# Moving a pair's second-layer weight loads to another queue, with four smaller reorderings around them

## Chip, cores and metric

The kernel runs on one core of a Trainium2 chip. The metric is the device time in microseconds of one execution; the times below are medians over repeated runs. The program's engines are TensorE (PE in the profile, its weight loads PEld), VectorE (DVE), ScalarE (ACT), GpSimd (POOL) and SyncE (SP). Transfers are issued from the queues of SP, POOL and, at the start, ACT.

## The reference

4096 tokens of width 256 pass a linear attention and a gated feed-forward block, each followed by a layer norm, in fp32:

```python
x = layernorm(x + attn(x))          # Q (K^T V) sqrt(3/D) Wo^T, D = 64
h = silu(x w1^T * s1) * (x w2^T * s2)        # 256 -> 1024
h = gelu(h h1^T * hs1)                        # 1024 -> 1024
h = gelu(h h2^T * hs2)                        # 1024 -> 1024
x = layernorm(x + (h w3^T) * s3)              # 1024 -> 256
```

The weights are ternary up to a scale.

## The kernel before

**Tiles and pairs.** The tokens are cut into 8 tiles of 512, and these are worked on in 4 pairs (tiles 0 and 1, 2 and 3, ...). An fp32 operand is split into a `hi` part (a cast, ScalarE) and a `lo` part (what the cast lost, VectorE), and TensorE runs every product twice, once with each. `convert` (L231, L232) does the split.

**A square layer.** The two 1024 x 1024 layers are computed for a pair at once by a scheme with 7 block products in place of 8 (`square_layer`). `product` issues 32 matmuls (L278) of 512 columns, about 7.25 us in all, into four PSUM banks: `al` or `be`. There are 14 products per pair, 7 per layer, counted in `products[0]` from 0. Their weight blocks are, in order, `A11, A12, S2, S1, S3, A22, S4`, each in two halves of 512 KB. `A11`, `A12` and `A22` are parts of the weight matrix itself; the `S` blocks are sums of its quarters. VectorE makes these sums once (`sums`, called per slice k = 0 to 3, in two halves `first` and `second`, through two rotating buffers named `so`), and POOL stores them into the DRAM arrays `sw` (L440). In the chain around a layer, `c11`, `c22` and `c12` add bank contents to a buffer on VectorE and apply a gelu on ScalarE; `c22` reads the four banks of `be` before product 6 adds to them.

**Weight queue.** `fetch` keeps up to five half blocks ahead (`HELD = 5`). For the first pair, `A` blocks of both layers come straight from the weight matrix on POOL's queue (L267); everything else comes from `sw` on SP's queue (L269). For the later pairs `copy` (L260) writes the `A` blocks from the matrix into `sw`, on SP's queue, after the products listed in `COPY`.

**Background work.** `fill(us)` gives out jobs from a list until a budget of microseconds is used up; a job may overdraw it, and what is overdrawn is taken from the next budget. The budgets of a layer are those after products 2, 3, 4 and 5 (`FIRST` in the first layer of the first pair, `FILL` elsewhere). In the first pair the list holds the sums of the second layer (`k0` to `k3`, two jobs of 1.4 each), for tiles 2 and 3 the normalisation (`a0, a1`, `b0, b1`, 1.3 each; statistics on VectorE, L167 on POOL) and the transposes (`a2, a3`, `b2, b3`, 0.8 each; VectorE, L815). `a3` and `b3` also put 32 small transfers into a list (`moves`, L216), which SP and POOL take in turn, up to 14 after each product.

**Around it.** Before the first pair, `stack_lo` (L550) makes the low parts of three stacked query tiles on POOL, and `attend_norm` normalises tiles 0 and 1 on VectorE (L167) with a root on POOL (L86). After each pair, `last_products` (L755) applies w3, and a dummy Silu on ScalarE fetches its table for the next pair. At the very end the kernel tests that its inputs are of the kind that it presumes (`within`, L863 and L864, a minimum, L998, and a matmul with ones, L1005), and branches on the outcome; the last normalisation is L1002.

[...]

Of the kernel before, what the change touches and what calls it, by code (L numbers as in the profile page):

```python
# [15 lines left out]
AF = mybir.ActivationFunctionType  # L16
ALU = mybir.AluOpType
AX = mybir.AxisListType
# [11 lines left out]
NP = NT // 2  # L30
NS = T // P
# [13 lines left out]
def block_kernel(ctx: ExitStack, tc: tile.TileContext, a: dict, out: bass.AP):  # L45
# [15 lines left out]
    nc = tc.nc  # L61
# [12 lines left out]
    mhalf = const("mhalf", [P, NS])  # L74
    once = const("once", [P, 1])
    ones = const("ones", [P, 1])
# [97 lines left out]
    def turn_on_pe(t, slot):  # L174

        hi, lo = slot
        j = t % 2

        def turn(s0, s1):
            for k in range(KE):  # L180
                for s in range(s0, s1):
                    nc.tensor.transpose(
                        aux[k][:, s * P : (s + 1) * P], x2[t][:, s, k * P : (k + 1) * P], ident
                    )

        def split(s0, s1):
            c = slice(s0 * P, s1 * P)
            for k in range(KE):
                h = hi[:, 2 * j + k, c]
                nc.scalar.copy(h, aux[k][:, c])  # L190
                nc.vector.tensor_tensor(  # L191
                    lo[:, 2 * j + k, c], aux[k][:, c], h.bitcast(F32), ALU.subtract
                )

        return turn, split
# [30 lines left out]
    def convert(src):  # L226

        hi, lo = next_slot()
        for h in range(2):
            c = slice(2 * h, 2 * h + 2)  # L230
            nc.scalar.copy(hi[:, c, :], src[:, c, :])  # L231
            nc.vector.tensor_tensor(  # L232
                lo[:, c, :], src[:, c, :], hi[:, c, :].bitcast(F32), ALU.subtract
            )
        return hi, lo

    MOVES = 14
    FILL = {2: 2.0, 3: 4.0, 4: 1.5, 5: 3.5}
    FIRST = {2: 2.8, 3: 5.4, 4: 2.8, 5: 5.4}

    PLACE = {A11: (0, 0), A12: (HK, 0), A22: (HK, T)}
    ORDER = [A11, A12, S2, S1, S3, A22, S4]
# [7 lines left out]
        return a[f"h{layer + 1}"][:, k0 : k0 + HK, c]  # L250


    copies = deque((layer, m, h) for layer in range(2) for m in PLACE for h in range(2))

    products = [0]
    COPY = (*range(8, 14), *range(15, 21))

    def copy():
        layer, m, h = copies.popleft()
        nc.sync.dma_start(out=sw[layer][m, h], in_=block(layer, m, h))  # L260

    def fetch(most=HELD):
        while wanted and len(held) < most:
            p, layer, m, h = wanted.popleft()
            w = p1.tile([P, HK, T // 2], FR, tag="ws", name=f"ws{m}", bufs=HELD)
            if p == 0 and m in PLACE:
                nc.gpsimd.dma_start(out=w, in_=block(layer, m, h))  # L267
            else:
                nc.sync.dma_start(out=w.bitcast(F32), in_=sw[layer][m, h])  # L269
            held.append(w)  # L270

    def product(ps, part, start):
        for h in range(2):
            w = held.popleft()
            for o in range(2):
                for k in range(HK):
                    for i in range(2):
                        nc.tensor.matmul(  # L278
                            ps[2 * h + o], w[:, k, o * P : (o + 1) * P], part[i][:, k, :],
                            start=start and k == 0 and i == 0, stop=k == HK - 1 and i == 1,  # L280
                            skip_group_check=True,
                        )
        fetch()
        products[0] += 1
        if products[0] in COPY:
            copy()
        move(MOVES)

    def plus(dst, u, v, op=ALU.add, engine=nc.vector):
# [2 lines left out]
    background = deque()  # L292
# [256 lines left out]
    def stack_lo(t):  # L549
        nc.gpsimd.tensor_tensor(  # L550
            stk[t][D:P], qf[t][D:P], stk[t][D:P].bitcast(F32), ALU.subtract
        )
# [3 lines left out]
    LATE = 6  # L556
# [42 lines left out]
    split(0, 2)  # L599
    norm(2)  # L600
    norm(3)
    for t in range(3, LATE):
        stack_lo(t)
    for t in range(LATE, NT):
        stack(t)

# [39 lines left out]
    for g in range(2):  # L646
        stats(g)
        root(g)
    turn, split = turn_on_pe(1, slot)
    for i in range(3, 2 * KH):  # L650
        for ps, w in zip(ring[i % 3], (w1, w2)):
# [8 lines left out]
        if i in (11, 14):  # L660
            t = 2 + i // 14
# [99 lines left out]
    def take(t, s, engine=nc.gpsimd):  # L761

        ps = (al, be)[t % 2][s]
        y = x2[t]
        d = p2.tile([P, E], F32, tag="d", name=f"d{t}", bufs=4)
        nc.vector.tensor_tensor(d, ps[:, :E], s3, ALU.mult)  # L766
        engine.tensor_tensor(y[:, s, :], y[:, s, :], d, ALU.add)  # L767
# [93 lines left out]
    def within(dst, var, so_far):  # L861

        nc.vector.tensor_scalar(dst, var, low, so_far, ALU.is_ge, ALU.mult)  # L863
        nc.vector.scalar_tensor_tensor(dst, var, high, dst, ALU.is_le, ALU.mult)  # L864
# [8 lines left out]
    for p in range(NP):  # L873
        ta, tb = 2 * p, 2 * p + 1
        if p > 0:
            first = []
            ask(1)
            for i in range(2 * KH):
                for ps, w in zip(ring[i % 3], (w1, w2)):
                    gate_products(ps, w, i % KH, slot, i // KH)  # L880
                if i == 0:
                    take(tb - 2, 0)
                    take(tb - 2, 1)
                if i == 1:
                    take(tb - 2, 2)
                    take(tb - 2, 3)
                gate(i, xb)
                if i in (2, 3, 5):
                    fill(1.2)
                if i in (4, 8):  # L890
                    first.append(convert(xb[0 if i == 4 else 2]))
                if p + 1 < NP and i in (6, 11):
                    t = ta + 2 + int(i == 11)
                    steps[t] = attend_norm(
                        t, xs[t], attention_out(t), (p2, late)[(p + 1) % 2]
                    )
                    steps[t][0](0)
                    steps[t][0](1)
                if i in (9, 10, 12, 13):
                    fill(1.2)  # L900
                if p == NP - 1 and i in (11, 13, 15):
                    bounds((i - 11) // 2)
        if p + 1 < NP:
            (a0, a1), (a2, a3) = attend_jobs(ta + 2)
            (b0, b1), (b2, b3) = attend_jobs(tb + 2)
            if p == 0:
                k0, k1, k2, k3 = (second_sums(k) for k in range(HK))
                background.extend((*k0, *k1, a0, a1, *k2, *k3, b0, b1, a2, a3, b2, b3))
            else:
                background.extend((a0, a1, b0, b1, a2, a3, b2, b3))  # L910
        tail = lambda: None
        for layer, sc in enumerate((hs1, hs2)):
            if p + layer > 0:
                ask(4 if p else 1)
            if p == NP - 1 and layer == 1:
                background.append((1.4, functools.partial(bounds, 3)))
            xb, first, tail = square_layer(
                xb, first, sc, tail, FILL if p + layer else FIRST
            )
        while background:  # L920
            background.popleft()[1]()
        if p + 1 < NP:
            nc.scalar.activation(once, mhalf[:, :1], AF.Silu)

        made = {}

        for s in range(NS):
            last_products(0, first[0], s)
        move(MOVES)
        tail()  # L930
        made[2] = convert(xb[3])
        for s in range(NS):
            last_products(1, first[1], s)
        move(MOVES)
        made[3] = convert(xb[1])
        for s in range(NS):
            take(ta, s)
        if p == NP - 1:
            break
        for i in (2, 3):  # L940
            for s in range(NS):
                last_products(i, made[i], s)
            if i == 2:
                move(len(moves))
                made[4] = convert(xTr)
        if p + 2 < NP:
            xs[ta + 4] = load_x(ta + 4)
            xs[tb + 4] = load_x(tb + 4)
        slot = made[4]
        xb = (xb[4], xb[5], xb[0], xb[2], xb[3], xb[1])  # L950
        background.extend(end_jobs(ta))
        background.extend(end_jobs(tb))
# [20 lines left out]
    g, v = nc.gpsimd, nc.vector  # L973
# [16 lines left out]
    for s in range(2):  # L990
        norm_on_act(tb, s, *rb[s])
    store(tb, 0, 2)
    take(tb, 3, v)
    rb.update(close(tb, [2]))
    norm_on_act(tb, 2, *rb[2])
    store(tb, 2, 3)
    within(ok[:, n - NS : n + 3], mvo[:, n - NS : n + 3, 1], fine)
    nc.vector.tensor_reduce(some, ok[:, : n + 3], AX.X, ALU.min)  # L998
    rb.update(close(tb, [3]))
    within(ok[:, n + 3 :], mvo[:, n + 3 :, 1], some)  # L1000
    y = x2[tb][:, 3, :]
    nc.vector.tensor_scalar(y, y, mvo[:, n + 3, 0:1], rb[3][1], ALU.subtract, ALU.mult)  # L1002
    store(tb, 3, 4)
    pf = bank[7][:1, :1]
    nc.tensor.matmul(pf, ok[:, n + 3 :], ones, start=True, stop=True)  # L1005
    nc.vector.tensor_scalar(flag, pf, float(P), None, ALU.is_lt)
    differs = nc.values_load(
        flag, engines=AGAIN, min_val=0, max_val=1,
# [156 lines left out]
```

## Time and profile before

| what | value |
| --- | --- |
| median of 3 runs | 652.41 us (651.53 to 653.03) |
| the profiled execution | 653.67 us, its span 651.9 us |
| TensorE busy | 631.8 us, 97% |
| VectorE, ScalarE, POOL busy | 496.1, 381.4, 233.1 us |
| DMA | 113.44 MB, mean 174 GB/s |

The span is the time from the first to the last instruction of the program, and the busy times are shares of it. In a row of instructions the columns are: start and length in us (timeline), or busy time in us, mean length of one in ns, and idle time before (groups); then engine, line and operation, what is written from what (buffer numbers left out), shapes, and the count. What stands in brackets, or behind `<-`, is what ended the idle time before. A row of the windows holds the window, its length, the busy time of the engine with its count of instructions, the granted TensorE clock as a share of full speed, the busy share of the DMA engines, and GB/s.

### The profile page before, as it was taken

To read this page: it belongs to the slowest core of one execution; us is meant where nothing else is said; L and a number is where in the kernel's file an instruction comes from. 1 tells how busy PE (TensorE), PEld (TensorE's weight loads), DVE (VectorE), ACT (ScalarE), POOL (GpSimd) and SP (SyncE) were. 2 spreads that over 40 slices of the span, in tenths; PEclk is the share of its full clock that TensorE was granted. 3 is DMA by queue.
4 is the path that set the end of the run, shared out by engine and by line. 5 is a ranking of instruction groups with operands and counts; after the bars stand their busy time and mean duration, and the time that the engine had idled before them with its cause. 6 is when DMAs were issued, how large, how long until landed. Compare 5 with 4: busy or idle time off the path is not lost.

```text
span 651.9 us, 8976 instructions
## 1 busy us (share of the span) xinstructions
PE 631.8 (97%) x3163; PEld 533.6 (82%) x3163; DVE 496.1 (76%) x750; ACT 381.4 (59%) x522; POOL 233.1 (36%) x290
## 2 busy tenths in 40 slices
PE   8999999959999999999999999999999999999994
PEld 7878888848898888888898888888899888888894
DVE  3789986895475888698677988798767987588466
ACT  5546472645664455655684556766684556766564
POOL 1234117722814713632535722631645720000005
PEclk9999999979999999999999999999999999999998
DMA  8988749845853037764762125654860125644201
GB/s 335 330 300 246 244 144 364 268 155 182 250 152 103 33 137 247 268 218 167 225 191 71 60 97 171 216 183 154 248 190 4 65 98 173 215 150 141 98 1 67
DMA packets 58800, 113.44 MB, mean 174 GB/s; under 512 B 19488, under 2 KB 34528, under 8 KB 58368
## 3 DMA queue, kind: packets, MB, share of 16 engines
q1 hardware_dynamic: 40864, 73.56, 34.0%
q0 software_dynamic: 17520, 38.55, 18.6%
q10 hardware_dynamic: 368, 0.72, 0.3%
q8 instruction: 26, 0.43, 0.3%
q14 instruction: 22, 0.18, 0.1%
HBM read 97.08 MB, written 18.87 MB: 178 GB/s over the span
## 4 chain that ended last, share of the span: by engine, by line
PE 86%; DMA 5%; DVE 5%; POOL 1%; issue 1%; ACT 1%; SPq 0%; POOLq 0%; DVEq 0%; ACTq 0%
PE bank L278 53%; PE bank L611 18%; PE bank L755 9%; DMA sw<-so 3%; PE bank L507 2%; DVE f L290 2%; PE bank L528 1%; DMA ws<-in_h 1%; POOL x L167 1%; DVE so L290 1%; DMA f<-in_xt 1%; PE bank L518 1%; PE bank L137 1%; PE bank L138 1%; DVE lo L232 1%
## 5 line engine op out<-in xcount | busy, mean ns | idle before, releaser
L278 PE MATMUL bank<-hi,ws 128*128 128x512 f32 x896 | 350.3, 391 | 7.7 <-DMA ws<-in_h 7.7
L278 PE MATMUL bank<-lo,ws 128*128 128x512 f32 x896 | 349.9, 391 | 0.0
L232 DVE TENSOR_TENSOR lo<-f,hi 128x1024 fp32r<-128x1024 f32 x144 | 170.3, 1221 | 69.6 <-ACT hi L231 69.1
L278 PEld LDWEIGHTS bank<-hi,ws 128*128 128x128 f32 x896 | 169.0, 189 | 43.3 <-DVE f L290 8.1
L278 PEld LDWEIGHTS bank<-lo,ws 128*128 128x128 f32 x896 | 169.1, 189 | 35.2
L231 ACT CAST hi<-f 128x1024 fp32r<-128x1024 f32 x144 | 144.5, 1051 | 52.0 <-PE bank L278 26.9
L318 ACT ACTIVATE f<-f,hs 128x512 f32<-128x512 f32 x96 | 62.8, 715 | 71.7 <-DVE f L290 71.7
L611 PE MATMUL bank<-hi,w 128*128 128x512 f32 (+1 forms) x268 | 101.7, 383 | 1.0 <-DVE d L766 0.6
L611 PE MATMUL bank<-lo,w 128*128 128x512 f32 (+1 forms) x268 | 101.2, 381 | 0.1
L620 ACT ACTIVATE f<-bank,s 128x512 f32<-128x512 f32 x64 | 44.0, 690 | 65.6 <-PE bank L611 62.3
L290 DVE TENSOR_TENSOR f<-f,f 128x1024 f32<-128x1024 f32 x64 | 76.5, 1221 | 4.5 <-ACT f L318 3.8
L290 DVE TENSOR_TENSOR f<-f,bank 128x512 f32<-128x512 f32 x96 | 62.1, 681 | 21.8 <-ACT f L371 16.0
L767 POOL TENSOR_TENSOR x<-x,d 128x256 f32<-128x256 f32 x31 | 27.0, 897 | 114.0 <-DVE d L766 113.9
L621 DVE SCALAR_TENSOR_TENSOR f<-bank,s,f 128x512 f32<-128x512 f32 x64 | 47.7, 748 | 26.2 <-PE bank L611 23.6
L755 PE MATMUL bank<-w,lo 128*128 128x256 f32 x256 | 61.6, 283 | 0.0
L755 PE MATMUL bank<-w,hi 128*128 128x256 f32 x256 | 61.6, 283 | 0.0
L611 PEld LDWEIGHTS bank<-hi,w 128*128 128x128 f32 x268 | 50.4, 188 | 11.3 <-DVE d L766 1.0
L611 PEld LDWEIGHTS bank<-lo,w 128*128 128x128 f32 x268 | 50.4, 188 | 9.6 <-DVE lo L191 0.3
L216 POOL DMA_DIRECT2D xT<-x x96 | 52.2, 551 | 8.1 <-DMA stage<-in_h 3.0
L755 PEld LDWEIGHTS bank<-w,lo 128*128 128x128 f32 x256 | 49.1, 192 | 0.2
L755 PEld LDWEIGHTS bank<-w,hi 128*128 128x128 f32 x256 | 49.1, 192 | 0.2
L717 POOL DMA_DIRECT2D stage<-in_h x16 | 9.0, 561 | 107.8 <-DVE stage L743 104.0
(121 smaller groups left out, 553.1 us busy)
## 6 DMA issues: line engine op xcount, KB each, us to landing
ws<-sw SPq DMA_DIRECT2D x100, 512.0 KB, 3.3
sw<-so POOLq DMA_DIRECT2D x16, 512.0 KB, 5.4
stage<-in_h POOLq DMA_DIRECT2D x16, 512.0 KB, 5.0
ws<-in_h POOLq DMA_DIRECT2D x12, 512.0 KB, 7.4
sw<-in_h SPq DMA_DIRECT2D x12, 512.0 KB, 5.5
x<-in_x SPq DMA_DIRECT2D x16, 256.0 KB, 3.7
f<-in_xt SPq DMA_DIRECT2D x6, 512.0 KB, 7.8
f<-in_h SPq DMA_DIRECT2D x6, 512.0 KB, 10.3
```

What stands on the lines that cost most here:

```text
L216: moves.popleft()()
L231: nc.scalar.copy(hi[:, c, :], src[:, c, :])
L232: nc.vector.tensor_tensor(lo[:, c, :], src[:, c, :], hi[:, c, :].bitcast(F32), ALU.subtract)
L278: nc.tensor.matmul(ps[2 * h + o], w[:, k, o * P : (o + 1) * P], part[i][:, k, :], start=start and k == 0 and i == 0, stop=k == HK - 1 and ...
L290: engine.tensor_tensor(dst, u, v, op)
L318: nc.scalar.activation(dst, src, AF.Gelu, scale=sc[:, o : o + 1])
L507: nc.tensor.matmul(pk[:, s, :], x[:, k, s * P : (s + 1) * P], wkv[:, k, :], start=(k == 0), stop=(k == KE - 1),)
L611: nc.tensor.matmul(ps[:, c], w[:, k, o * P : (o + 1) * P], part[:, 2 * j + k, c], start=(k == 0 and i == 0), stop=(k == KE - 1 and i == 1),)
L620: nc.scalar.activation(g, pa, AF.Silu, scale=s1[:, o : o + 1])
L621: nc.vector.scalar_tensor_tensor(g, pb, s2[:, o : o + 1], g, ALU.mult, ALU.mult)
L755: nc.tensor.matmul(ps[:, :E], part[q][:, k, s * P : (s + 1) * P], w3[:, k0 + k, :], start=i % 2 == 0 and k == 0 and q == 0, stop=i % 2 == ...
L767: engine.tensor_tensor(y[:, s, :], y[:, s, :], d, ALU.add)
```

## The change

- For the first pair, only the first layer's `A` blocks come on POOL's queue; the second layer's come from `sw` on SP's queue. The copies of the second layer are made first, and copies are given out at the start of products 0, 1, 2, 5, 7 to 12, 14 and 15.
- The budgets `FIRST` rise from 2.8 / 5.4 to 3.2 / 5.8, and in the list the transposes of tile 2 (`a2, a3`) stand ahead of the normalisation of tile 3 (`b0, b1`).
- `stack_lo` is issued behind the root of tile 1.
- The dummy Silu is issued behind `tail`, the last gelu of the pair.
- At the end, the last add of tile 3 is issued behind tile 2's normalisation and store, and the tests of the last tile are made in one step in place of two.

```diff
-    FIRST = {2: 2.8, 3: 5.4, 4: 2.8, 5: 5.4}
+    FIRST = {2: 3.2, 3: 5.8, 4: 3.2, 5: 5.8}
...
-    copies = deque((layer, m, h) for layer in range(2) for m in PLACE for h in range(2))
+    copies = deque((layer, m, h) for layer in (1, 0) for m in PLACE for h in range(2))
...
-    COPY = (*range(8, 14), *range(15, 21))
+    COPY = (0, 1, 2, 5, *range(7, 13), 14, 15)
...
-            if p == 0 and m in PLACE:
+            if p + layer == 0 and m in PLACE:
                 nc.gpsimd.dma_start(out=w, in_=block(layer, m, h))
...
     def product(ps, part, start):
+        if products[0] in COPY:
+            copy()
...
         products[0] += 1
-        if products[0] in COPY:
-            copy()
         move(MOVES)
...
     norm(3)
-    for t in range(3, LATE):
-        stack_lo(t)
     for t in range(LATE, NT):
         stack(t)
...
     for g in range(2):
         stats(g)
         root(g)
+    for t in range(3, LATE):
+        stack_lo(t)
...
-                background.extend((*k0, *k1, a0, a1, *k2, *k3, b0, b1, a2, a3, b2, b3))
+                background.extend((*k0, *k1, a0, a1, *k2, *k3, a2, a3, b0, b1, b2, b3))
...
-        if p + 1 < NP:
-            nc.scalar.activation(once, mhalf[:, :1], AF.Silu)
-
         made = {}
...
         tail()
+        if p + 1 < NP:
+            nc.scalar.activation(once, mhalf[:, :1], AF.Silu)
...
     store(tb, 0, 2)
-    take(tb, 3, v)
     rb.update(close(tb, [2]))
     norm_on_act(tb, 2, *rb[2])
     store(tb, 2, 3)
-    within(ok[:, n - NS : n + 3], mvo[:, n - NS : n + 3, 1], fine)
-    nc.vector.tensor_reduce(some, ok[:, : n + 3], AX.X, ALU.min)
+    take(tb, 3, v)
     rb.update(close(tb, [3]))
-    within(ok[:, n + 3 :], mvo[:, n + 3 :, 1], some)
+    within(ok[:, n - NS :], mvo[:, n - NS :, 1], fine)
+    nc.vector.tensor_reduce(some, ok, AX.X, ALU.min)
...
-    nc.tensor.matmul(pf, ok[:, n + 3 :], ones, start=True, stop=True)
+    nc.tensor.matmul(pf, some, ones, start=True, stop=True)
```

## The prediction, made before the changed kernel was run

> **What bounds the kernel now.** I read the page first (TensorE busy 97% of the span, so only what it waits for can be won), then the waits of TensorE:
>
> ```profile
> engine line waited for: us in total, times, longest us
> PE bank L278 <- DMA ws<-in_h: 7.7, 1, 7.7
> ...
> PE bank L182 <- DVE x L167: 0.7, 1, 0.7
> PE bank L611 <- DVE d L766: 0.6, 1, 0.6
> ```
>
> One wait matters: 7.7 us for a weight block (`ws<-in_h`, the loads on POOL's queue). The chain over 90 to 143 us tells why it is late:
>
> ```profile
> 115.93 5.08 DMA sw<-so
> ...
> 125.85 3.83 POOL x L167 x2
> ...
> 134.19 7.89 DMA ws<-in_h
> ...
> 142.21 1.19 PE bank L278 x2
> ```
>
> The load was queued on POOL behind tile 3's normalisations (L167) and issued only at 134.19. TensorE's windows show a second price:
>
> ```profile
> 136.00:137.00 1.00, 0.00 (x0) 1.00 0.88 287
> 137.00:138.00 1.00, 0.00 (x0) 0.52 1.22 337
> 143.00:147.00 4.00, 4.00 (x10) 0.50 0.02 4
> 147.00:148.00 1.00, 1.00 (x5) 0.86 0.00 0
> ```
>
> The granted clock (third figure) fell to half some 2.6 us into the wait and came back at about 147.3. The chain has 42.54 us for the 176 matmuls after the wait; at the 101.55 us that it has for 448 elsewhere, they take 39.9. So the wait costs 7.7 + 2.7 = 10.4 us. Two further readings decide what replaces it. VectorE's timeline:
>
> ```profile
> 112.84 0.69 DVE L290 TENSOR_TENSOR so<-xT 128x512 fp32r<-128x512 f32 x1 [0.98 <-DMA sw<-so]
> 113.44 0.69 DVE L290 TENSOR_TENSOR so<-xT,so 128x512 fp32r<-128x512 f32 x1
> 114.05 2.47 DVE L290 TENSOR_TENSOR f<-f,bank 128x512 f32<-128x512 f32 x4
> ...
> 121.13 0.69 DVE L290 TENSOR_TENSOR so<-stk 128x512 fp32r<-128x512 f32 x1 [0.47 <-DMA sw<-so]
> ```
>
> and POOL's:
>
> ```profile
> 106.32 1.63 POOL L86 TENSOR_TENSOR ra<-ra,mhalf 128x2 f32<-128x2 f32 x1
> ...
> 111.81 3.34 POOL L167 TENSOR_SCALAR x<-x,mv,ra 128x256 f32<-128x256 f32 x2
> 115.09 0.84 POOL L267 DMA_DIRECT2D ws<-in_h  x1
> 115.93 1.51 POOL L440 DMA_DIRECT2D sw<-so  x2
> ```
>
> The rows at 114.05 are `c22`, which reads the banks `be`; TensorE starts product 6, which writes them, at 116.2 (72.66 + 6 x 7.25), only 1.5 us after `c22(0)`. The row at 121.13 is the first half of the sums of k=3, waiting for the store of k=2 to free its buffer. That store left POOL at 115.93, behind tile 2's normalisations, and landed 5.08 us later.
>
> **Weights by copies.** Six POOL loads (0.75 to 0.9 us of issue, 7.4 us to landing) become SP loads (0.32 us, 3.3 us to landing). The copies they need go out at products 0, 1, 2, 5, 7, 8, and each lands in about 5.5 us (median of the 12); each is read at least one product (7.25 us) later. A12's second half can be issued when its buffer is free (about 120) instead of 134.19, and is wanted at 134.3. The 10.4 us go. What is late next in that line is S2 of this layer, which needs the sums of k=3 stored: wanted at product 9, not close. Extra traffic: three copies at about 69, 80 and 88 us, where the DMA engines are half busy (0.51 over 80 to 100), one at 109, where they are full.
>
> **Larger budgets.** `FIRST` of 3.2 / 5.8 lets `fill` give out: k0, k0, k1 after product 2; k1, tile 2's two norm jobs, k2 after product 3; k2 **and the first half of k3** after product 4; k3, both transposes of tile 2, both norm jobs of tile 3 and, by the rounding of the remainder, the first transposes of tile 3 after product 5. The half of k3 thus moves ahead of `c22`. It cannot start before k2's first store has landed:
> - k1's first half waits for the store landing at 100.65 as now, but the two `lo` of t4 (2.3 us) now stand behind it; k1's second half ends at about 105.7 instead of 104.1. POOL issues its store and two raw loads by 107.8 (now 106.3).
> - Tile 2's norm jobs take 8.8 us of POOL now (106.32 to 115.09), partly in VectorE's way; I take 7.6, since VectorE will stand still for their end: k2's store leaves at 115.4. Landing is 5.1 us now and 3.4 at the least for such stores; with the copy and three loads on SP's queue beside it I take 5.0: 120.4.
> - k3's half takes 1.4, `c22(0)` 0.7: TensorE starts product 6 at 122.6, not 116.2, a new wait of 6.4 us (bounds: 4.0 with 114.5 and 3.6; 8.0 with 116.6 and 5.5).
> - The clock: 2.7 us again. The Trainium skill (TensorE: Matmul & The Clock Gate, What's actually happening) says about 3.4 us of work restore it, which would be 1.7; the row has 5.1 us (142.2 to 147.3), and I use the row.
>
> Queued behind the half of k3 on VectorE: `c22`, the `lo` of n1, k3's other half, four transposes (0.33 each), tile 3's statistics, two transposes that wait for POOL's first norms of tile 3 (about 2.7), the `lo` of n2, `c12`, `both`, t2. Adding the rows' durations from the landing at R: `lo` of t2 ready and the first bank copied at R + 27.8, product 9 wants them at R + 26.5; `c11(0)` ends at R + 36.0, product 10 wants it at R + 35.1. Two more waits, 1.3 + 0.9 = 2.2 us (bounds 0 and 5).
>
> This part: -10.4 + 6.4 + 2.7 + 2.2 = **+0.9**.
>
> **Order on POOL of A22 and k1's store.** A22's second half now goes out behind k1's first store (103.2 instead of 98.95). By the queue's order they swap landings: 110.4 instead of 108.9; wanted at 112.5. Nothing; 1 us if the queue is slower.
>
> **Transposes of tile 2 ahead.** 32 small DMAs, 16 on each of POOL (0.55 us) and SP (0.6 us), 7 of each per product from product 6: about 4 us of 7.25 on each queue. SP's loads run four blocks ahead, which hides them (without that lead a block would come up to 4 us late); at the handover to pair 1, the xT wait goes that held ACT, then VectorE's L766, then TensorE by 0.6: **-0.6** (0 to -0.6). The Silu load behind `tail` saves two table loads of 1.28 us on ACT, none of which TensorE waits for: nothing.
>
> **`stack_lo` later.** Now, at 37.4 us:
>
> ```profile
> 37.44 2.75 DVE L167 TENSOR_SCALAR x<-x,mv,ra 128x256 f32<-128x256 f32 x2
> ...
> 50.38 1.45 DVE L167 TENSOR_SCALAR x<-x,mv,ra 128x256 f32<-128x256 f32 x4
> ```
>
> Two normalisations took 2.75 us beside the three `stack_lo` on POOL (37.47 to 41.3), while four took 1.45 at 50.38. Moving POOL's work away saves TensorE its waits of 0.74 and 0.18 at 40 us: -0.9. But it lands at 50.6, right behind POOL's root of tile 1 (49.88 + 0.69), where those four run, and TensorE's transposes follow at 51.44. The Trainium skill (SBUF — State Buffer, Who interferes with whom) speaks against this: the pair of ports is locked for a whole instruction and issue order decides. If VectorE, which starts at 50.38, kept it through, nothing would be lost; but at 37.44 VectorE started 30 ns ahead and still lost, so by the row three of the four wait 1.3 us each and the last ends at 54.7 instead of 51.9: +2.8. I take +2.8; the clock should hold, since four transposes are strewn in. Sum **+1.9** (bounds -0.9 and +4.6, with a drop of the clock).
>
> **Tail.** Tile 3's add (643.50) moves behind four small operations of tile 2 (about +0.3), and three test operations and a statistics pass leave its path. Summing the same rows: the last normalisation starts at 646.3 instead of 647.41: **-1.1** (-0.5 to -1.4).
>
> **Sum:** +0.9 - 0.6 + 1.9 - 1.1 = +1.1. The profiled execution took 653.67 us (span 651.9), 1.3 above the median of 652.41; I set the change on the median: **653.5**.
>
> **Rivals.** (a) The new wait does not come, because k2's store is out before POOL's norms: -10.4 - 0.6 + 1.9 - 1.1 = -10.2, 642.2. Against it: the jobs are given out in order, and the trace has that store at 115.93, its data ready since 111.9. 8%. (b) The wait is short and `stack_lo` meets nothing: 4.1 + 2.7 + 1.0 - 10.4 - 0.9 - 0.6 - 1.1 = -5.2, 647.2. For it: idle stretches have stores of 3.4 us. 25%. (c) Slower: VectorE's backlog. It is 0.9 us late at product 10 already, so every further microsecond counts whole; if two norms of tile 3 take 3.8 us (as at 125.85) and the `lo` beside POOL 1.4 each, it is some 4 us more: 657.5. It decides as soon as `c11(0)` ends later than R + 35. 18%. The traded wait itself: 49%, own range 650.5 to 656.
>
> **Numbers.** 0.2% (1.3 us) is about what can be told from no change. Faster: (a), (b) and 5 of the trade, 38%; within: 20%; slower: 24 of the trade and (c), 42%. The range 646 to 659 leaves out (a), the low end of (b) and the high end of (c).
>
> **What would show it.** Right: no `ws<-in_h` wait; a wait of TensorE of about 6 us near 118 on VectorE's f (L290), with the clock at half; VectorE idle before that on `sw<-so`; POOL's L550 at 50.6 with long L167 beside it; L1002 a microsecond nearer to the last matmul. Wrong: `c22` on time near 116, which would give (a).

## The result, and the profile after

The changed kernel is slower: 661.94 us (median of 4 runs, 660.35 to 664.76) against 652.72 for the kernel before in the same job, a ratio of 1.0139 with a 95% interval of 1.0091 to 1.0188. The forecast was 653.5, with a range of 646 to 659. The profiled execution of the changed kernel took 660.35 us, its span is 658.6 (before: 653.67 and 651.9).

First the row where most of the miss lies, which neither the chain nor the table of waits shows: the closing instructions of the program, listed by the program's last line for POOL and for SP. DRAIN is the name of instructions that the profile shows at the end of each queue. The columns are line, queue, operation and count, then shortest, median and longest duration in ns, and the first and last start in us. Of the kernel before:

```profile
L1160 POOLq DRAIN  x3: 46/103/4273, 646.8 to 651.6; - x3
L1160 SPq DRAIN  x3: 7/7/13, 650.7 to 651.3; - x3
```

and of the changed kernel:

```profile
L1158 POOLq DRAIN  x3: 46/103/9782, 648.0 to 658.3; - x3
L1158 SPq DRAIN  x3: 7/7/7, 651.9 to 658.0; - x3
```

POOL's longest DRAIN took 4.27 us before and 9.78 us now. For its last 5.7 us nothing else runs, as the windows of the changed kernel show (window, length, busy time and count of PE, PEld, DVE, ACT and POOL, granted clock, DMA share, GB/s):

```profile
650.00:652.00 2.00, 0.00 (x0) 0.00 (x0) 0.00 (x0) 0.00 (x0) 0.00 (x0) 0.50 0.23 71
652.00:654.00 2.00, 0.00 (x0) 0.00 (x0) 0.00 (x0) 0.00 (x0) 0.00 (x0) 0.50 0.00 0
654.00:656.00 2.00, 0.00 (x0) 0.00 (x0) 0.00 (x0) 0.00 (x0) 0.00 (x0) 0.50 0.00 0
656.00:658.00 2.00, 0.00 (x0) 0.00 (x0) 0.00 (x0) 0.00 (x0) 0.00 (x0) 0.50 0.00 0
```

The last data land at 650.75, SP's own closing work ends at 652.01, and then all engines stand until the DRAIN ends at 657.75.

Before that point the waits of the changed kernel are of the kinds that the prediction named; their sizes come below. The waits of TensorE:

```profile
PE bank L280 <- DVE f L290: 7.4, 1, 7.4
...
PE bank L182 <- DVE x L167: 2.4, 3, 0.9
...
PE bank L280 <- ACT f L347: 0.9, 1, 0.9
...
PE bank L280 <- issue: 0.6, 1, 0.6
```

The 7.7 us wait for `ws<-in_h` is gone; in its place stands the wait of product 6 for `c22` (L290), with two small ones behind it (ACT f and issue). The chain over this stretch (start, length, what) has the steps in the order that the prediction gave:

```profile
115.02 0.89 POOL x L167
115.92 0.75 issue
116.66 6.00 DMA sw<-so
...
122.78 0.70 DVE so L290
...
124.12 0.69 DVE f L290
124.81 0.04 issue
124.85 17.45 PE bank L280 x64
```

Tile 2's last normalisation on POOL, then the store of k2, then VectorE's half of k3 that waits for it, then `c22(0)`, then product 6. The clock (third figure, TensorE alone) was at half by then, and came back 5.6 us into the work:

```profile
121.00:122.00 1.00, 0.00 (x0) 0.50 1.06 430
...
129.00:130.00 1.00, 1.00 (x4) 0.50 0.00 0
130.00:131.00 1.00, 1.00 (x5) 0.77 0.00 0
```

The next table gives the start of each stage in the two profiles, in us.

| point | before | after | shift |
| --- | --- | --- | --- |
| first gate product | 36.79 | 36.50 | -0.28 |
| gate product 60 | 48.70 | 46.90 | -1.80 |
| product 0 | 72.66 | 73.72 | +1.06 |
| product 6 | 116.19 | 124.85 | +8.67 |
| product 7 | 123.44 | 134.87 | +11.43 |
| product 10 | 155.58 | 158.69 | +3.11 |
| product 14 (pair 1) | 231.84 | 234.20 | +2.36 |
| last w3 matmul | 643.18 | 645.54 | +2.36 |
| last normalisation | 647.41 | 648.62 | +1.21 |
| POOL's DRAIN ends | 651.06 | 657.75 | +6.68 |
| span ends | 651.88 | 658.56 | +6.68 |

At the last normalisation the shift is +1.21, against a predicted sum of +1.1. The remaining 5.5 us come after it. The agreement of the first figure is luck, as the sections below show: it comes from one pair of profiles, in which several terms happened to fall well.

### The profile page after: what moved, and what is told of

The parts are those of the page before. It is cut to its first block, busy times and chain, and to the rows that moved or that the text cites. A ratio compares the mean times of both kernels' runs of the same rounds, so it can differ in the third digit from the quotient of the medians.

```text
span 658.6 us, 8962 instructions
## 1 busy us (share of the span) xinstructions
PE 632.3 (96%) x3163; PEld 533.9 (81%) x3163; DVE 496.9 (75%) x748; ACT 373.1 (57%) x516; POOL 228.4 (35%) x284
## 4 chain that ended last, share of the span: by engine, by line
PE 86%; DMA 5%; issue 3%; DVE 3%; POOL 1%; SPq 0%; ACT 0%; DVEq 0%; POOLq 0%
PE bank L280 55%; PE bank L609 16%; PE bank L755 9%; PE bank L507 2%; DMA sw<-so 2%; PE bank L528 1%; DMA x<-in_x 1%; DMA xT<-x 1%; DMA f<-in_xt 1%; PE bank L518 1%; DVE x L167 1%; POOL x L167 1%; PE bank L137 1%; PE bank L138 1%; DMA ws<-sw 0%
## 5 line engine op out<-in xcount | busy, mean ns | idle before, releaser
L318 ACT ACTIVATE f<-f,hs 128x512 f32<-128x512 f32 x96 | 62.7, 715 | 85.5 <-DVE f L290 85.5
L290 DVE TENSOR_TENSOR f<-f,f 128x1024 f32<-128x1024 f32 x64 | 76.4, 1220 | 4.5 <-ACT f L318 3.8
L290 DVE TENSOR_TENSOR f<-f,bank 128x512 f32<-128x512 f32 x96 | 61.8, 681 | 18.9 <-ACT f L371 13.7
## 6 DMA issues: line engine op xcount, KB each, us to landing
w<-in_w POOLq DMA_DIRECT2D x3, 1024.0 KB, 10.6
```

The lines of the kernel that those rows point to most:

```text
L290: engine.tensor_tensor(dst, u, v, op)
L318: nc.scalar.activation(dst, src, AF.Gelu, scale=sc[:, o : o + 1])
```

## The experiments

**The larger budgets.** The changed kernel with the old `FIRST`:

```diff
-    FIRST = {2: 3.2, 3: 5.8, 4: 3.2, 5: 5.8}
+    FIRST = {2: 2.8, 3: 5.4, 4: 2.8, 5: 5.4}
```

> The changed kernel with the budgets FIRST put back to 2.8 / 5.4. Theory (the first half of k3's sums stands before c22 and waits for k2's store): VectorE's f (L290) is no longer waited for near 118 us, so 7.6 us of wait and 2.8 us of half clock go; the last w3 matmul of pair 0 comes 8 to 11 us sooner than in the changed kernel, the total falls from about 662 to 651 to 654. Rival (the wait near 118 comes from the earlier copies crowding the DMA engines): the wait stays above 4 us and the total stays above 658. On the long DRAIN of POOL at the end (9.8 us in the changed kernel, 4.3 before): no part of it is touched here, so it should stay near 10 if anything in the weights' queue or the tail makes it.

Measured: 652.55 us, ratio to before 0.9999 (0.9975 to 1.0023). The wait for `c22` is gone. From product 0 to product 9 this kernel takes 66.9 us; the changed kernel took 76.7, so the larger budgets alone cost some 10 us (one profile each). Yet it is not faster than the kernel before, although its last w3 matmul comes 3.6 us earlier and its last normalisation 4.7: its DRAIN is 9.78 us too.

**The weight loads alone.** The kernel before with the three edits of the weights (order of `copies`, `COPY` at the start of a product, loads of the second layer from `sw`), and nothing else:

```diff
-    copies = deque((layer, m, h) for layer in range(2) for m in PLACE for h in range(2))
+    copies = deque((layer, m, h) for layer in (1, 0) for m in PLACE for h in range(2))
...
-            if p == 0 and m in PLACE:
+            if p + layer == 0 and m in PLACE:
```

> The kernel before with only the weights' part: second layer's A blocks from copies on SP's queue, new order and places of the copies. Theory: the 7.7 us wait for ws<-in_h and its half clock (2.7) go and nothing takes their place in the first layer, so the last w3 matmul of pair 0 comes about 10 us sooner than before, the total is 642 to 644 with a short DRAIN. Rival 2 (fewer POOL transfers lengthen the DRAIN): the same body but a DRAIN near 10, total 646 to 649. Rival (the copies' traffic delays the sums): a new wait of over 3 us on VectorE or on ws<-sw.

Measured: 652.6 us, ratio 1.0003 (0.9988 to 1.0017). The body gained 5.7 us (last w3 matmul at 637.46, not 643.18), and the DRAIN took it back:

```profile
L1160 POOLq DRAIN  x3: 46/103/9742, 641.1 to 651.4; - x3
```

So the long DRAIN comes with the weight edits, without the tail, the budgets or `stack_lo`.

**The tail, both ways.** The changed kernel with the old tail, and the kernel before with the new one:

```diff
     store(tb, 0, 2)
+    take(tb, 3, v)
...
-    take(tb, 3, v)
```

(and the two test steps in place of one, as in the change's diff, read backwards for the first kernel and forwards for the second).

> The changed kernel with the old tail (tile 3's add early, tests in two steps, matmul on ok). Theory 1 (the new tail lengthens POOL's closing DRAIN): DRAIN back to about 4.3 us, total 3 to 5 us below the changed kernel although the last normalisation comes 1.1 us later after the last w3 matmul. Rival 2 (six POOL transfers fewer do it): DRAIN stays near 10 and the total is 1 us above the changed kernel's where the DRAIN does not hide it. Rival 3 (chance): neither length is bound to the kernel.

> The kernel before with nothing but the new tail. Theory 1 (new tail lengthens the DRAIN): DRAIN near 10 us, total 4 us above before. Rival 2 (POOL transfers): DRAIN near 4, the last normalisation 1.1 us sooner after the last w3 matmul and the total 1 us below before. Rival 3 (chance): any DRAIN.

Measured: 664.08 us (1.0183, 1.0147 to 1.0219) and 651.76 us (0.9988, 0.9965 to 1.0011). From the last w3 matmul to the last normalisation it is 4.23 us with the old tail and 3.07 with the new one, in both kernels: the tail is worth its 1.15 us at that point. In the whole time of the second kernel it is not clear of the noise. The DRAIN is 9.74 in the first and 4.31 in the second, so the tail is not its cause.

**`stack_lo` behind the first split.** The old `FIRST`, and POOL's `stack_lo` issued later, behind the loads of the weights:

```diff
-    for t in range(3, LATE):
-        stack_lo(t)
...
             split(0, 4)
+            for u in range(3, LATE):
+                stack_lo(u)
```

> The changed kernel with the old assignment of the stack_lo jobs after the first split at the 36 to 52 us stretch moved behind it, and FIRST back at 2.8 and 5.4. Four runs so far show POOL's closing DRAIN at 9.6 to 9.8 us wherever the six weight loads left POOL's queue, and at 4.1 to 4.3 where they did not. Body theory: no wait before product 6, stack_lo off the gates, so the last w3 matmul at about 636 to 638. If the DRAIN is set by the traffic on POOL's queue (queue theory): DRAIN 9.8, time 646 to 649. If the DRAIN is long by chance of a build (rival): DRAIN 4 to 10, time 641 to 649. If stack_lo was not what cost the front (rival): about 652, as with FIRST put back alone.

Measured: 647.97 us, ratio 0.9929 (0.9906 to 0.9953). VectorE's rows (start, length) show the difference. In the changed kernel, whose `stack_lo` starts at 48.91:

```profile
48.58 4.31 DVE L167 TENSOR_SCALAR x<-x,mv,ra 128x256 f32<-128x256 f32 x4
```

In this kernel, with `stack_lo` at 51.91:

```profile
48.57 1.44 DVE L167 TENSOR_SCALAR x<-x,mv,ra 128x256 f32<-128x256 f32 x4
```

The four normalisations take 2.87 us more beside `stack_lo`. Against the first experiment, which differs from this kernel in the place of `stack_lo` alone, the ratio to before falls from 0.9999 to 0.9929. The 1.5 us that the change won before gate product 60 are kept (shift -1.82, -1.62 at product 0). DRAIN 9.78 again.

**What POOL's queue has to do with it.** To the kernel of the last experiment a few transfers that serve nothing are added on POOL's queue behind the last staging load, near 555 us: four or three of a weight block, or six of one element.

```diff
             next_check.done += 1
+            if next_check.done == len(pieces):
+                for j in range(4):
+                    nc.gpsimd.dma_start(out=extra[j], in_=block(0, A11, j % 2))
```

> The same kernel with four more transfers of a weight block (DRAM to DRAM, of no use to the result, about 528 packets each) issued on POOL's queue after the last staged load near 560 us: about 16460 packets and 163 transfers on that queue. Packets theory with a ring that wraps between 14352 and 17520 packets[...]: DRAIN falls to 4 to 5 us, the time 5 us under the kernel without them. Packets theory without a wrap, more packets a shorter DRAIN: about 6.5 us. Count theory (165 transfers short, 159 long): between or long. Chance or place of the code: DRAIN as without them, 9.8.

> The same kernel with three more transfers of a weight block on POOL's queue: about 15940 packets, below 16384. Packets theory with a wrap at 16384: DRAIN long, 9.8 to 10.5 us. Packets theory without a wrap: about 7.3 us. Count theory: between or long.

> The same kernel with six more transfers of one element each on POOL's queue at the same place: 165 transfers as in the kernel before, but only about 100 packets more. Count theory: DRAIN back to 4.3 us, time 5.5 us under the kernel without them. Packets theory: DRAIN stays at 9.8 us, time unchanged.

Measured: 644.13, 644.02 and 650.18 us (ratios 0.9858, 0.9856 and 0.9959), with DRAINs of 1.62, 1.54 and 10.28 where the kernel without them had 9.78. The rows of three more blocks and of six tiny ones:

```profile
L1163 POOLq DRAIN  x3: 46/103/1537, 637.6 to 642.2; - x3
```

```profile
L1163 POOLq DRAIN  x3: 46/103/10276, 637.3 to 648.1; - x3
```

More traffic made the DRAIN 8 us shorter in two kernels and 0.5 us longer in one. The blocks came out at 144 packets each, not the 528 that I had reckoned with. A plain "more transfers, longer DRAIN" fails, and so does a plain "fewer, longer", and so does a wrap at 16384 packets: the queue of the kernel with three blocks more had 14784.

**The test of the cause.** The changed kernel exactly as it is, except that the last four loads of weights of the last pair go on POOL's queue, which has nothing else to do then:

```diff
-                nc.sync.dma_start(out=w.bitcast(F32), in_=sw[layer][m, h])
+                late = p == NP - 1 and layer == 1 and m in ORDER[-2:]
+                queue = nc.gpsimd if late else nc.sync
+                queue.dma_start(out=w.bitcast(F32), in_=sw[layer][m, h])
```

> The changed kernel as it is, with only the last four loads of weight copies on POOL's queue. Its body stays (last w3 matmul 2.4 us behind the kernel before); DRAIN 1.6 instead of 9.8, and the end then set by SP's closing work, so about 6 us less than the changed kernel: 655 to 657. If the DRAIN is not set by that queue's traffic: 661 to 663.

Measured: 657.17 us, ratio to before 1.0069 (1.0045 to 1.0094), 4.8 us under the changed kernel's median.

```profile
L1160 POOLq DRAIN  x3: 46/103/1452, 650.9 to 655.4; - x3
L1160 SPq DRAIN  x3: 7/7/13, 654.8 to 655.1; - x3
```

The wait for `c22` is there as before (8.1 us), the long DRAIN is not. It ends at 652.33, and SP's closing work at 654.89 now sets the end. This shows that the missing 5.5 us are POOL's DRAIN, and that what was issued on POOL's queue sets its length. No useless transfer is needed. It shows as well what the rest of the change costs: with a short DRAIN the kernel is still 0.7% slower than before, some 4.5 us, and not the 1.1 us that were predicted.

**The best version.** The same four loads on POOL's queue, with the old `FIRST` and `stack_lo` behind the split:

> The version with FIRST back and the stack_lo jobs behind the first split, and with the last four loads of weight copies of the last pair (144 packets each) on POOL's queue, where nothing else is due then: 14928 packets there, as in the run with four more transfers. Theory that POOL's work at the end grows with the transfers since a restart about every 7300 packets (estimate from five DRAINs: before 4.3, changed 9.8, +6 tiny 10.3, +3 blocks 1.5, +4 blocks 1.6): DRAIN 1.6 us, time 642 to 644. Rival, that it was the useless transfers as such (DRAM to DRAM) that shortened it: DRAIN 9.8, time 648. If the loads come late on POOL's queue: a wait before one of the last four products, 644 to 648.

Measured: 643.09 us (642.16 to 644.34), ratio 0.9857 (0.9835 to 0.988). DRAIN 1.45 us, the last normalisation 10.6 us earlier than in the kernel before, the end 11.0 us. It beats both kernels. TensorE's largest waits within the layers are now 1.0, 0.8 and 0.7 us.

**When does the DRAIN fall back?** From the first runs I had an estimate: POOL's work at the end grows with the transfers since some restart, a point from which the count begins anew, and which comes about every 7300 packets. Two kernels tested it on the kernel before: its 23 staging loads on SP's queue in place of POOL's, and 36 more thin transfers on POOL's.

```diff
-        nc.gpsimd.dma_start(out=st[:, :n], in_=src.rearrange("p k o -> p (k o)")[:, c : c + n])
+        nc.sync.dma_start(out=st[:, :n], in_=src.rearrange("p k o -> p (k o)")[:, c : c + n])
```

> The kernel before, with its 23 staging loads (for the tests of the weights) on SP's queue instead of POOL's: 14304 packets and 142 transfers on POOL's queue, almost the packets of the changed kernel, with the weight loads untouched. Restart theory: some 110 transfers since the last restart against 46, so the DRAIN about 9 us instead of 4.3, and the time 4 to 5 us up apart from waits that the staging loads may cause on SP's queue. If only the weight loads matter: DRAIN 4.3.

```diff
+            if next_check.done == len(pieces):
+                for j in range(36):
+                    nc.gpsimd.dma_start(out=extra[0, :, 0, j : j + 1], in_=block(0, A11, 0)[:, 0, j : j + 1])
```

> The kernel before with 36 more useless transfers of 128 elements of 4 B each (144 packets each) on POOL's queue after the last staging load: 22704 packets. Restart theory (restarts near 7300, 14600 and 21900): DRAIN 1.6 to 2.2 us, and the time 1 to 3 us under the kernel before. If the DRAIN simply grows with the transfers beyond 14600 packets: 7 us, time 2 to 3 us over it.

Measured: 651.16 us (0.9991, 0.9972 to 1.0009) with a DRAIN of 2.38, and 654.5 us (1.0039, 1.002 to 1.0059) with one of 7.22. The first contradicts the estimate, which gave 9. The 36 transfers of the second came out at 32 packets each, so no restart was due by packets, and the DRAIN grew by 2.94 us: 82 ns for each transfer, as 6 tiny ones had given (0.50) and the fourth block (0.08).

Three single runs came from that: 40 tiny transfers or three blocks in the version with the old `FIRST` and `stack_lo` behind the split, and 90 tiny ones in the kernel before. The three blocks were meant to have 528 packets each, but came out at 144 again (14784 on the queue), so this run repeats the earlier one with three blocks.

> The version with FIRST back and stack_lo behind the first split, with 40 more transfers of one element (32 packets each) on POOL's queue near 555 us. DRAIN was 9.78 us without, 10.28 with 6 such, 1.54 with 3 of 144 packets. If packets decide the restart: it comes with the 7th to 13th of them, and 27 to 33 transfers behind it at 82 ns give 3.7 to 4.2 us. If the number of transfers decides (2 or 3 more were enough with larger ones, 6 tiny were not): no restart, 9.78 + 40 x 0.082 = 13.1 us. In both, the last w3 matmul stays where it was.

> The same version with three more transfers of 528 packets (1 KB pieces) instead. Packets theory: the restart comes with the first, two behind it: DRAIN 1.6 us. A theory in which only the number counts gives 1.5 to 10 us as the three of 144 packets gave 1.5.

> The kernel before with 90 more one-element transfers on POOL's queue after the last staging load. DRAIN was 4.27 us without and 7.22 with 36 of 32 packets. If the restart needs some 7000 packets since the last one (before stands at about 2100 to 3000, 90 more add 2880): none, and 4.27 + 90 x 0.082 = 11.7 us. If it comes after about 105 to 110 transfers whatever their size (before stands at about 34): it comes within these 90, and 14 to 19 behind it give 2.6 to 3.0 us.

Measured DRAINs: 3.58, 1.54 and 1.74 us (643.96, 641.76 and 649.95 us, one run each). The fall comes within the 40 and within the 90. POOL's timeline of the 40 tiny ones shows where (start, length, group, and in brackets the idle time before it and what ended it):

```profile
555.87 2.50 POOL L838 DMA_DIRECT2D extra<-in_h  x5 [0.70 <-DMA stage<-in_h]
560.75 13.99 POOL L838 DMA_DIRECT2D extra<-in_h  x28 [2.38 <-issue]
```

POOL pauses 2.38 us in its issuing, waiting for nothing that the profile shows, and 28 transfers follow. The kernel before has such a pause, with 37 transfers from it to the end:

```profile
458.62 1.63 POOL L216 DMA_DIRECT2D xT<-x  x3 [1.88 <-issue]
```

and the changed kernel has one with 104:

```profile
172.43 3.81 POOL L216 DMA_DIRECT2D xT<-x  x7 [0.93 <-issue]
```

With n transfers since the pause, 1.26 + 0.082 n us gives (an estimate; the slope is that of the 36 transfers, the constant was set to fit; the pause is the last one of at least 0.8 us):

| kernel | n since the pause | estimate | DRAIN |
| --- | --- | --- | --- |
| before | 37 | 4.29 | 4.27 |
| changed | 104 | 9.79 | 9.78 |
| six tiny more | 110 | 10.28 | 10.28 |
| three blocks more | 3 | 1.51 | 1.54 |
| changed, last four loads on POOL | 2 | 1.42 | 1.45 |
| before, 36 more | 73 | 7.25 | 7.22 |
| 40 tiny more | 28 | 3.56 | 3.58 |
| before, 90 tiny more | 6 | 1.75 | 1.74 |

In the test of the cause the pause comes before the third of the four loads:

```profile
614.51 0.53 POOL L271 DMA_DIRECT2D ws<-sw  x1 [5.68 <-issue]
```

Eight of the nine other kernels agree to 0.05 us: those with 104 transfers since the pause (`FIRST` back, old tail, weights alone, `stack_lo` later) have DRAINs of 9.74 to 9.78, the new tail in the kernel before (37) has 4.31, four blocks (4) 1.62, the second run of three blocks (3) 1.54, the best version (2) 1.45. The ninth does not: the kernel with the staging loads on SP's queue has 103 transfers since its last such pause, which would make 9.7, and a DRAIN of 2.38; that would fit n = 14, where its trace shows no pause. So the count describes these traces, with one exception; no kernel's DRAIN was forecast with it. Which pauses count was also found from the DRAINs: one of 0.42 us in the changed kernel, at 309.20, does not begin the count anew.

The changed kernel ends 104 transfers after its pause, and so does the version with the old `FIRST` and `stack_lo` later. With blocks added there, the next pause came before the first of them; with tiny transfers, only behind the twelfth. So the changed kernel ends shortly before a next pause, and the four loads of the test carried it over one. What brings the pause stays open. Between the last two pauses lie 104 transfers (three blocks more), 106 (the test), 116 (40 tiny) and 121 (before, 90 tiny), with 4880 to 6848 packets, so neither is constant; earlier in the programs some lie closer, 88 transfers in the kernel before.

## Why the prediction was wrong

**The weights by copies: right, and too large.** The wait went, as said. Its worth was taken from one profile, 10.4 us from product 0 to 9. The four later profiles of the kernel before with an unchanged first pair (new tail, staging on SP, 36 and 90 more) take 73.2, 73.6, 74.6 and 73.0 us over this stretch, not 75.7. Against the 65.3 that nine products need, the wait and the half clock were worth 7.8 to 9.3 there, and 10.4 in the profile that the prediction was made from. What varied is the one load: TensorE went on 8.0 us after its issue there, and 5.3 to 7.8 us after it in the four.

**The larger budgets: right in every step, low in size.** k2's store left at 116.66 (predicted 115.4), landed in 6.0 us (5.0), and product 6 started at 124.85 (122.6, or 123.7 with the shift of +1.06 at product 0): a wait of 7.4 us, not 6.4, within the bound of 8.0; 8.5 and 8.1 us in the two further kernels that keep these budgets, just past it. The clock cost 2.76 us at product 7 (predicted 2.7). The half clock lasted 10.24 us in both profiles (137.04 to 147.28 before, 120.23 to 130.47 now), and 6.83 or 3.41 us in the layers and gate products of other kernels, so in steps of some 3.41 us. From the first matmul after the wait to the full clock it was 5.1 us before and 5.6 now. The Trainium skill (TensorE: Matmul & The Clock Gate, What's actually happening) gives about 3.4 us, as the length of a window that runs free of the work; taken as the time to the full clock it would have made the loss 1.7. The row was the better basis.

The later waits, before products 9 and 10, are 2.1 us by the starts of the products (predicted 2.2). But they do not come from the budgets, under which the prediction has them: the kernels with the old `FIRST` show 2.6 (`FIRST` back), 2.4 (weights alone) and 2.4 us (`stack_lo` later) at the same two places. They stand behind the wait for the weight block, and appear when it goes. The weight edits alone therefore bring some 6 us from product 0 to product 10 (75.6 and 75.1 us, against 81.3 as the mean of five profiles before), and the budgets then cost some 10.

Taking the means of several profiles, the way from product 0 to product 10 is 81.3 us before (five profiles) and 85.5 with the change (three): +4.2, where this part of the sum said +0.9. In the pair of single profiles it was only +2.05. The terms that were mis-sized are the wait that goes (10.4 for some 8.7) and the wait that comes (6.4 for some 8).

**A22 and k1's store: within its doubt.** A22's second half landed at 112.85, not 110.4; wanted half way through product 5, which is at 113.6 here (109.99 + 3.63), it held nothing up.

**`stack_lo`: right in kind; its size was met by luck.** Up to gate product 60 the change won 1.5 us (predicted 0.9), and from there to product 0 it lost 2.9 (predicted 2.8). The row at 37.44 held: VectorE's first normalisation took 0.40 us and was over when `stack_lo` had just begun; the other three took 1.35 to 1.44 us each, the first of them although it started 0.01 us ahead of `stack_lo`. "The clock should hold" did so in this profile. In the three others with this edit the clock fell to half for 3.41 us, and the loss was 4.3 to 4.5, near the upper bound. The windows of the kernel with `FIRST` back, TensorE alone:

```profile
54.00:55.00 1.00, 0.33 (x1) 1.00 0.00 0
55.00:56.00 1.00, 0.52 (x3) 0.53 0.00 0
56.00:57.00 1.00, 1.00 (x5) 0.50 0.64 96
```

Over the four profiles the edit costs 2.5 us from the first gate product to product 0, not 1.9.

**Transposes ahead: right in this pair of profiles.** 0.75 us from product 10 to 14 (predicted 0.6, from 0 to 0.6). In the other profiles of the kernel before with the old order this stretch takes 76.5 us once and 75.6 three times, against 75.5 with the change, so the gain is 0.1 to 1.0 from profile to profile.

**The tail: right.** 1.15 us (predicted 1.1), in every profile.

**The end: the step that failed.** "Summing the same rows: the last normalisation starts at 646.3 instead of 647.41" took it that all behind the last normalisation is fixed, so that what is won there is won at the end. No term stood for POOL's DRAIN. Yet the prediction itself counted that six POOL loads become SP loads. In the trace of before, SP's closing work ended at 650.77 and the DRAIN at 651.06, so the DRAIN already set the end by 0.3 us; the closing row, L1160, was not read. How far it would grow could not be worked out from that trace, but that the end hangs on POOL's queue, from which the change takes six transfers, could be read there, and calls for a term with a wide bound. Its 5.5 us are the largest part of the miss of 8.4, and without them the time would lie within the range. The test shows this: the changed kernel with a short DRAIN took 657.17. The rest is the trade above (3.3 us on the means) and `stack_lo` (0.6), which are together more than is left; single profiles do not settle it closer.

**The rivals.** (a) and (b) failed, since the store left behind POOL's normalisations as the queue's order has it. (c), the VectorE backlog, did not decide: products 9 and 10 together started 2.1 us late, about as the trade had it. Its time, 657.5, was the nearest, by luck: the DRAIN made up for it, which it did not name.

## What to carry to other kernels

A transfer moved from one queue to another can change more than the wait that it was moved for: list what the last line of the program does on each queue, see which of them ends last, and give it a term. In these kernels POOL's closing work jumped by up to 8 us when the count of transfers on its queue changed by a few. And a wait whose length hangs on transfers should be sized from more than one profile before a gain is set on it.

## What was not expected of the hardware

POOL's closing DRAIN took between 1.45 and 10.28 us in these kernels; each further transfer on POOL's queue lengthened it by 82 ns, whether of 32 packets or of 144. Behind a pause in POOL's issuing (0.8 to 2.5 us, and one row of 5.7 in the kernels that load weights there) it fell to 1.45 to 1.62 with two to four transfers left. What brings the pause is not known, and one kernel does not fit. With the DRAIN short, SP's closing work sets the end, 4.15 us behind the last normalisation in place of 9.94.

A VectorE normalisation that overlapped POOL's `stack_lo` took 1.35 to 1.44 us in place of 0.40, also where it had started 0.01 us first.

The half clock of TensorE lasted 3.41, 6.83 or 10.24 us each time that it came and went before the end of the program.

The start of the first gate product varied from 36.4 to 39.2 us between profiles, also in unchanged code, and the wait in product 8 with its half clock by 2.6 us in unchanged code. In single profiles, differences of 2 us in the first pair therefore say little.
